# Constant rows in PSUM, six more gathered groups and one counted block less in a graph layer

## The chip, the cores and the metric

The kernel runs on one core of a Trainium2 chip. Its time is the device time of one execution in microseconds; a figure for a kernel is the median of several runs. A profile is one more execution, taken by the hardware profiler: its span runs from the first instruction to the last, and the execution itself is a little longer than that. Engines are named as in the profile: PE is TensorE (PEld its weight loads), DVE is VectorE, ACT is ScalarE, POOL is GpSimd, SP is SyncE, which issues most DMAs.

## What is computed

One graph layer with a residual. There are 6250 nodes of 64 features and 206250 edges, sorted by target node; W1 is 64x128, W2 is 128x64, all in float32.

```python
h = jnp.maximum(_layernorm(x, axis=-1), 0.0)
...
msg = node_feat[src] + edge_feat
agg = jax.ops.segment_sum(msg, dst, num_segments=node_feat.shape[0])
h = jax.nn.relu(agg @ W1 + b1)
return h @ W2 + b2
...
x = x + _L0_gnn_ref(h, edge_attr_64, src, dst, ...)
```

`node_feat` is the normalised `h` here. Each node has some 33 edges. The sum over edges of `h[src]` is the heavy part: it touches 206250 rows of `h` in no order.

## The kernel before

**Two ways to the sum of h.** For most nodes the kernel doesn't fetch rows of `h`. It counts: for a window of three nodes (128 slots of edges, `SLOTS`) it makes a matrix of how often each source node occurs, by a product of two matrices of ones and zeros. A source number is split into a low part (0 to 127) and a key (a high part, 49 values, beside which of the three nodes is meant, so `K` = 147 columns). `hot_lo` says which low part an edge has, `hot_key` which key; VectorE makes both by comparing the edges' numbers with a row of consecutive numbers, `iota_lo` and `iota_key` (line 858). TensorE multiplies them into `pc` in PSUM (line 868), and ScalarE moves `pc` to the ring of counts in SBUF (line 871). Then TensorE multiplies the counts by `h` itself, held in SBUF in 49 pieces, into `pv` (line 888), and VectorE adds `pv` to the sums of all nodes, `agg` (line 900).

For the last groups of edges (a group is 1024 edges) GpSimd gathers rows of `h` from a table in HBM by indirect DMAs (line 301), 128 rows each, which add the rows to the edges' own features in the tile `pfeat`; eight gathers make a group. There are `GP` = 20 such groups; they are worked in pairs. TensorE sums a pair by node (line 489) with a matrix of ones and zeros (`hotp`), ScalarE empties it, TensorE places it (line 508), and VectorE adds it to `agg` (line 473).

**Steps and blocks.** The counts run in steps: six windows in one step (`ST`), so six matmuls and one eviction. 14 steps are a block (84 windows, 252 nodes), and there are `NW` = 23 blocks, the last with `BL` = 56 windows (10 steps): 318 steps. Every third step opens a new pair of `hot_lo` and `hot_key`, with 18 windows each, in two buffers. In the first seven steps of a block the 49 products of the block before are dealt out, 5 to 8 a step (`PRODUCTS`); in step 11 they are added (`ADDED`). `pv` has two buffers in PSUM, `pc` two of two banks each, `bank` and `po` one each: all eight banks are used.

**Feature sums.** The edges' own features are summed apart, in chunks of 42 nodes, two chunks to a unit, three units to a block, behind the counts of steps 8, 11 and 14 (`SUMS`). VectorE makes `hot` a step ahead (line 427), 48 matmul records on TensorE sum the unit in `bank` (line 439), ScalarE empties it into `by_node` (line 442), which frees the features' buffers for the next load, and TensorE adds it to the next block's open `pv` (line 461). The layer for a block of 252 nodes (`mlp_hidden` and what follows) is dealt out over later steps.

**Order.** The order on every engine is the order in which the program records it; nothing reorders it later. A planner in the program decides behind which step a pair of gathered groups is summed. It has two clocks of its own: one of steps (`clock`, 1.25 us a step, `STEP_US`), one of GpSimd (`pool`, 2.3 us a gather by `GATHER_US`, 2.9 a fetch of words by `WORDS_US`). A pair is recorded in the first step of a block among 1, 2, 3 and 5 (`GROUPS`) where GpSimd's clock plus `LAND_US` is over. Four `pfeat` tiles hold two pairs, so the gathers of a pair wait until the pair two before it is summed. If the gathers come later than the planner has them, TensorE waits at the sum, with all that stands behind it.

**The opening.** Before the first step, the edges' sources are converted on ScalarE (line 589), transposed on TensorE (594), evicted (595) and packed with the targets by VectorE (598), then written to HBM. The first edges of each window are found by a search over gathered rows (lines 311 and 317). `by_quarters` turns the sources of the gathered groups for the gathers' indices, through `pv`'s buffers (651, 653): one quarter, then two, then the last ahead of the counts of step 4.

Of the kernel before, what the change touches and what calls it, by code (L numbers as in the profile page):

```python
# [55 lines left out]
GP = 20  # L56
# [20 lines left out]
NW = 23  # L77
BL = 56
# [32 lines left out]
GATHER_US = 2.3  # L111
WORDS_US = 2.9
# [9 lines left out]
def gnn_kernel(ctx: ExitStack, tc: tile.TileContext, x, src_t, dst_t, dst_g, edge, w1, b1, w2, b2, out):  # L122
# [278 lines left out]
    nc.vector.memset(bank, 0.0)  # L401
    units = []
# [29 lines left out]
    def chunk_sum(u):  # L432
        n = units[u][2]
        hot, feat = hot_of.pop(u), feats.pop(u)
        for i in range(n):
            for k in range(JP):
                for q in range(JQ):
                    j = q * JP + k
                    nc.tensor.matmul(bank[q * QP:q * QP + WQ, i * D:(i + 1) * D], hot[:, i, j, :], feat[i][:, j, :],  # L439
                                     start=(k == 0), stop=(k == JP - 1))  # L440
        by_node[u] = work.tile([P, GB, D], F32, name="by_node", bufs=3)
        nc.scalar.activation(by_node[u][:, :n].rearrange("p c d -> p (c d)"), bank[:, :n * D], AF.Copy)  # L442
        load(u + 2)
# [201 lines left out]
    def by_quarters(t0, t1):  # L645
        rows = src_s.bitcast(F32)
        for t in range(t0, t1):
            own = slice(t * QP, (t + 1) * QP)
            px = ps.tile([P, 512], F32, tag="pv", name="psrcq")[:, :GP * PK]
            for b in range(PQ):  # L650
                nc.tensor.matmul(px, spread[own, b].rearrange("p a c -> p (a c)"), rows[own, :, b, :],
                                 start=(b == 0), stop=(b == PQ - 1))
            nc.scalar.activation(src_p[:, :, t], px.rearrange("p (g k) -> p g k", k=PK), AF.Copy)
# [31 lines left out]
    junk = late.tile([P, RC * CT], BF16, name="junk")  # L685
# [159 lines left out]
    def count(b, s):  # L845
# [4 lines left out]
        if r == 0:  # L850
# [5 lines left out]
            for k, (hot, iota_k) in enumerate(zip(hots, (iota_lo, iota_key))):  # L856
# [18 lines left out]
    def open_pv(b):  # L875
        pvs[b] = [ps.tile([P, 512], F32, tag="pv", name="pv")[:, :BN], 0]
# [102 lines left out]
    def fetch_h(g):  # L979
# [4 lines left out]
        for j in range(J):  # L984
            queue.append((GATHER_US, lambda j=j: gather(
# [116 lines left out]
    PRODUCTS_L = (8, 18, 28, 39, HI)  # L1102
    ADDED, LOADED = 10, 2
    LAST, LATE, SUMS_L = (3, 8), 7, (6, 8)
# [13 lines left out]
    places = {}  # L1118


    for u, (b, c, _) in enumerate(units):
# [4 lines left out]
        at(n, chunk_sum, u)  # L1126
# [15 lines left out]
    for n, (b, s) in enumerate(steps):  # L1142
        for f in before.get(n, []):
            f()
        count(b, s)
# [3 lines left out]
        if b >= 1 and s == (PLACES if b < NW - 1 else 2):  # L1149
# [23 lines left out]
        if n >= 3:  # L1173
            if h_next < G and s in GROUPS and fetched.get(h_next + 1, 1e9) + LAND_US <= clock(n):
# [164 lines left out]
```

## Time and profile before

| | |
|---|---|
| median of 3 runs | 492.47 us (490.9 to 494.97) |
| profiled execution | 489.07 us |
| its span | 487.2 us |
| PE busy | 424.2 us, 87% |
| DVE busy | 415.1 us, 85% |
| POOL busy | 388.3 us, 80% |
| ACT busy | 366.0 us, 75% |
| DMA moved | 77.98 MB, 160 GB/s over the span |

TensorE's busy time is modelled: matmuls are pipelined, and records of one matmul overlap. An f32 matmul shows as two records. In rows of groups the columns are line, engine, operation, what is written from what, shapes and count, then busy us and mean ns of one, then the engine's idle time just before them with what ended most of it. In rows of the timeline they are the start and duration in us, then the same, with the idle time just before and its end in brackets.

### The profile page before, as it was taken

Reading aid. Unit: us, or ns where it says so; the run is one execution under the profiler, and the core shown is the slowest. Engines: PE = TensorE matmul, PEld = TensorE weight load, DVE = VectorE, ACT = ScalarE, POOL = GpSimd, SP = SyncE. Lnnn points to the kernel's source line nnn. Section 1 sums busy time; section 2 is a strip of 40 time slices with the busy share of each in tenths; the row PEclk is TensorE's granted clock in tenths of the full one; section 3 lists DMA queues with packets and bytes.
Section 4 is the critical chain, followed back from the end, with each engine's and each line's share of the span. In section 5 each row is a group of like instructions: output and inputs, shape, how many; then the busy total and the mean of one; then the engine's idle time right before and its main releaser. Section 6 shows DMA issues by size and latency. Waiting matters only on the chain.

```text
span 487.2 us, 17218 instructions
## 1 busy us (share of the span) xinstructions
PE 424.2 (87%) x7301; PEld 374.8 (77%) x7302; DVE 415.1 (85%) x561; ACT 366.0 (75%) x607; POOL 388.3 (80%) x239
## 2 busy tenths in 40 slices
PE   3156798998988999999999999989999999999894
PEld 3055687886886888888988978878888888888783
DVE  7888989879999798988998889888998899998751
ACT  3727889878877788788898789777887787786650
POOL 7787888888888888888888888888888888888000
PEclk9655699999999999999999999999999999999998
DMA  9959367378366585784784784675775775764700
GB/s 237 238 172 300 74 147 193 76 180 192 69 167 155 145 228 122 176 230 105 192 220 98 172 228 94 170 201 125 187 187 124 201 179 122 203 158 93 213 13 16
DMA packets 122378, 77.98 MB, mean 160 GB/s; under 512 B 34768, under 2 KB 120728, under 8 KB 122072
## 3 DMA queue, kind: packets, MB, share of 16 engines
q1 hardware_dynamic: 97464, 66.88, 47.1%
q0 software_dynamic: 24592, 9.19, 15.0%
q8 instruction: 59, 0.97, 0.8%
q10 hardware_dynamic: 240, 0.75, 0.5%
q14 instruction: 23, 0.19, 0.1%
HBM read 72.80 MB, written 3.99 MB: 158 GB/s over the span
## 4 chain that ended last, share of the span: by engine, by line
PE 68%; ACT 13%; DMA 6%; issue 5%; DVE 4%; POOL 3%; DVEq 0%; ACTq 0%; POOLq 0%
PE pv L888 26%; PE pc L868 22%; PE bank L439 11%; ACT counts L871 9%; POOL rows L301 3%; DMA feat<-in_edge 3%; PE po L943 2%; PE pv L461 2%; DMA dstq<-in_dst_g,cols_i 2%; ACT junk L694 1%; PE ph L936 1%; PE bank L489 1%; DVE hot_key L858 1%; DVE hot_lo L858 1%; DMA firsts_i<-in_dst_g 1%
## 5 line engine op out<-in xcount | busy, mean ns | idle before, releaser
L301 POOL DMA_INDIRECT pfeat<-table,src_p x160 | 334.0, 2088 | 49.7 <-issue 43.0
L871 ACT ACTIVATE counts<-pc 128x882 fp32r<-128x882 f32 x318 | 282.1, 916 | 49.1 <-PE pc L868 39.8
L868 PE MATMUL pc<-hot_key,hot_lo 128*128 128x147 bf16 x1908 | 179.2, 232 | 22.9 <-ACT counts L871 13.6
L858 DVE TENSOR_TENSOR hot_lo<-iota_lo,keys 128x2304 bf16<-128x2304 bf16 (+1 forms) x107 | 143.8, 1344 | 36.2 <-PE pc L868 29.0
L888 PE MATMUL pv<-counts,h 128*128 128x252 f32 (+1 forms) x1127 | 171.0, 292 | 0.2
L868 PEld LDWEIGHTS <-hot_lo 128*128 128x128 bf16 x1908 | 130.5, 100 | 45.4 <-issue 24.2
L858 DVE TENSOR_TENSOR hot_key<-iota_key,keys 128x2664 bf16<-128x2664 bf16 (+1 forms) x107 | 163.3, 1526 | 0.0
L888 PEld LDWEIGHTS pv<-counts,h 128*128 128x128 f32 x1127 | 143.5, 190 | 0.6 <-ACT counts L871 0.5
L439 PE MATMUL bank<-feat,hot 128*21 128x64 f32 x3240 | 69.0, 222 | 5.9 <-issue 3.0
L439 PEld LDWEIGHTS bank<-feat,hot 128*21 128x21 f32 x3240 | 52.3, 101 | 18.3 <-issue 6.8
L427 DVE TENSOR_TENSOR hot<-rel,iota 128x504 f32<-128x504 bf16 x68 | 45.6, 671 | 0.1
L442 ACT ACTIVATE by_node<-bank 128x128 f32<-128x128 f32 x68 | 19.0, 280 | 18.4 <-PE bank L439 12.4
L301 POOL DMA_INDIRECT words<-packed,first_i x15 | 20.8, 1385 | 4.6 <-issue 3.4
L301 POOL DMA_INDIRECT rows<-in_dst_g,row_i x15 | 17.4, 1162 | 5.2 <-issue 4.0
L943 PE MATMUL po<-w2s,hid 128*126 128x64 f32 (+2 forms) x100 | 16.8, 288 | 1.7 <-ACT hid L938 1.2
L943 PEld LDWEIGHTS po<-w2s,hid 128*126 128x126 f32 (+2 forms) x100 | 13.5, 192 | 5.7 <-ACT hid L938 1.9
L936 PE MATMUL ph<-sums,w1s 128*128 128x252 f32 (+2 forms) x50 | 16.1, 404 | 0.2 <-ACT y L949 0.2
L900 DVE TENSOR_TENSOR sums<-sums,pv 128x252 f32<-128x252 f32 (+4 forms) x31 | 9.8, 339 | 6.7 <-PE pv L888 5.9
L492 ACT ACTIVATE by_group<-bank 128x128 f32<-128x128 f32 x10 | 2.8, 277 | 15.1 <-PE bank L489 11.1
L938 ACT ACTIVATE hid<-ph,b1s 128x252 f32<-128x252 f32 (+2 forms) x25 | 11.6, 464 | 2.3 <-PE ph L936 2.3
L461 PE MATMUL pv<-select,by_node 128*64 128x42 f32 (+1 forms) x272 | 12.6, 234 | 0.0
L461 PEld LDWEIGHTS pv<-select,by_node 128*64 128x64 f32 x272 | 9.9, 137 | 3.0
(202 smaller groups left out, 252.3 us busy)
## 6 DMA issues: line engine op xcount, KB each, us to landing
feat<-in_edge SPq DMA_DIRECT2D x135, 384.0 KB
pfeat<-in_edge SPq DMA_DIRECT2D x20, 256.0 KB
pfeat<-table,src_p POOLq DMA_INDIRECT x160
xl<-in_x SPq DMA_DIRECT2D x2, 768.0 KB
xs<-in_x SPq DMA_DIRECT2D x23, 63.0 KB
out_y<-y SPq DMA_DIRECT2D x23, 63.0 KB
dstn<-in_dst_g SPq DMA_DIRECT2D x1, 1024.0 KB
table<-xl SPq DMA_DIRECT2D x1, 800.0 KB
```

The source lines that it names most:

```text
L301: nc.gpsimd.indirect_dma_start(out=rows, out_offset=None, in_=source, in_offset=bass.IndirectOffsetOnAxis(ap=index, axis=0), compute_op=op)
L427: nc.vector.tensor_tensor(hot_of[u][:, :n].rearrange("p c j w -> p (c j) w"), rel[:, c:c + n].rearrange("p c q k -> p (c q k)").unsqueeze( ...
L439: nc.tensor.matmul(bank[q * QP:q * QP + WQ, i * D:(i + 1) * D], hot[:, i, j, :], feat[i][:, j, :], start=(k == 0), stop=(k == JP - 1))
L442: nc.scalar.activation(by_node[u][:, :n].rearrange("p c d -> p (c d)"), bank[:, :n * D], AF.Copy)
L461: nc.tensor.matmul(pvs[b][0][i * D:(i + 1) * D, k:k + z - a], of[:, i, :], select[:, a - low:z - low], start=False, stop=False)
L858: nc.vector.tensor_tensor(hot[:, :n].rearrange("p t (m o) -> p t m o", o=2), iota_k.rearrange("p (m o) -> p m o", o=2).unsqueeze(1).to_bro ...
L868: nc.tensor.matmul(pc[:, k, m * K:(m + 1) * K], hot_lo[:, j, :], hot_key[:, j, :K], start=True, stop=True)
L871: nc.scalar.activation(ring[:, (2 * b + half) % 3, :, i * ST * V:(i + 1) * ST * V].rearrange("p h (k m) -> p h k m", k=2), pc[:, :, :ST // ...
L888: nc.tensor.matmul(pv[:, :2 * half].rearrange("p (k n) -> p k n", k=2), h2[:, h, :], of[:, :, h, :half], start=(h == 0), stop=(h == HI - 1))
L936: nc.tensor.matmul(ph[:, :n], w1s, agg[:, start[b]:start[b + 1]], start=True, stop=True)
L938: nc.scalar.activation(outs[b][:, :n], ph[:, :n], AF.Relu, bias=b1s)
L943: nc.tensor.matmul(po[:pairs[b], k, :], outs[b][:, k:2 * pairs[b]:2], w2s, start=True, stop=True)
```

## The change

**Constant rows.** A new PSUM tile `iotas` (bf16, one bank) holds the two rows of consecutive numbers that line 858 compares with. It is filled once, near the start: a matmul spreads a row over a column, ScalarE copies it to SBUF, a transpose puts it back as a row on all partitions; this three times. The comparisons then read `iotas` in PSUM in place of `iota_lo` and `iota_key` in SBUF. For its bank, `pv` goes from two buffers to one, in `open_pv` and in `by_quarters`.

**More gathered, fewer counted.** `GP` goes from 20 to 26, `NW` from 23 to 22 with the last block full (`BL` 84): 308 steps. Gathers whose edges all lie past the end of the list are left out (four, in the last group): 204 gathers in place of 160. `GATHER_US` goes from 2.3 to 1.6, `WORDS_US` from 2.9 to 1.2. A pair may also be summed in any step of the last block after the third. The last block's places for products, sums and layers become those of the other blocks, or later.

**Feature sums.** A unit's first chunk is summed ahead of its step's counts, the second where both were, behind them.

In the built program the 13 pairs stand behind 43, 58, 85, 100, 127, 143, 169, 187, 211, 229, 253, 271 and 295 steps; before, the ten stood behind 47, 85, 113, 142, 173, 211, 239, 271, 309 and the last in the drain.

```diff
-GP = 20
+GP = 26
...
-NW = 23
-BL = 56
+NW = 22
+BL = 84
...
-GATHER_US = 2.3
-WORDS_US = 2.9
+GATHER_US = 1.6
+WORDS_US = 1.2
...
     bank = ps.tile([P, GB * D], F32, name="bank", bufs=1)
     nc.vector.memset(bank, 0.0)
+    iotas = ps.tile([P, P + K + 1], BF16, name="iotas", bufs=1)
+    col = ps.tile([P, 3, P], F32, tag="pc", name="pcol")
+    cols_of = late.tile([P, 3, P], BF16, name="iota_cols")
+    m = K + 1 - P
+    for k, of in enumerate((iota_lo, iota_key[:, :P], iota_key[:, P:])):
+        n = of.shape[1]
+        nc.tensor.matmul(col[:n, k, :], of[0:1, :], onesb[0:1, :], start=True, stop=True)
+        nc.scalar.activation(cols_of[:n, k, :], col[:n, k, :], AF.Copy)
+        nc.tensor.transpose(iotas[:, k * P:k * P + n], cols_of[:n, k, :], identb[:n, :n])
...
-    def chunk_sum(u):
+    def chunk_sum(u, i):
         n = units[u][2]
-        hot, feat = hot_of.pop(u), feats.pop(u)
-        for i in range(n):
+        hot, feat = hot_of[u], feats[u]
+        if i < n:
             for k in range(JP):
...
+        if i < GB - 1:
+            return
+        hot_of.pop(u)
+        feats.pop(u)
         by_node[u] = work.tile([P, GB, D], F32, name="by_node", bufs=3)
...
-            px = ps.tile([P, 512], F32, tag="pv", name="psrcq")[:, :GP * PK]
+            px = ps.tile([P, 512], F32, tag="pv", name="psrcq", bufs=1)[:, :GP * PK]
...
-            for k, (hot, iota_k) in enumerate(zip(hots, (iota_lo, iota_key))):
+            for k, (hot, iota_k) in enumerate(zip(hots, (iotas[:, :P], iotas[:, P:]))):
...
-        pvs[b] = [ps.tile([P, 512], F32, tag="pv", name="pv")[:, :BN], 0]
+        pvs[b] = [ps.tile([P, 512], F32, tag="pv", name="pv", bufs=1)[:, :BN], 0]
...
         for j in range(J):
+            if g * P * J + j // PK * P * PK + j % PK >= E:
+                continue
...
-    PRODUCTS_L = (8, 18, 28, 39, HI)
+    PRODUCTS_L = PRODUCTS
     ADDED, LOADED = 10, 2
-    LAST, LATE, SUMS_L = (3, 8), 7, (6, 8)
+    LAST, LATE, SUMS_L = (5, 12), 11, SUMS
...
-        at(n, chunk_sum, u)
+        sum_first.setdefault(n, []).append(u)
+        at(n, chunk_sum, u, 1)
...
+        for u in sum_first.pop(n, []):
+            chunk_sum(u, 0)
         count(b, s)
...
-            if h_next < G and s in GROUPS and fetched.get(h_next + 1, 1e9) + LAND_US <= clock(n):
+            if h_next < G and (s in GROUPS or b == NW - 1 and s > LOADED) and fetched.get(h_next + 1, 1e9) + LAND_US <= clock(n):
```

More of the change, by code (lines that the diff above doesn't have):

```diff
@@ L684, in gnn_kernel @@
     sums_bad = bad[:, CHECKED + 2 * NT:]
-    junk = late.tile([P, RC * CT], BF16, name="junk")
+    junk = late.tile([P, max(RC * CT, 2 * GP * J)], BF16, name="junk")
     def checked(of, p, low, high, at):
@@ L1118, in gnn_kernel @@
     places = {}
+    sum_first = {}
     for u, (b, c, _) in enumerate(units):
@@ L1148, in gnn_kernel @@
             multiply(b - 1, upto[s])
-        if b >= 1 and s == (PLACES if b < NW - 1 else 2):
+        if b >= 1 and s == PLACES:
             for u in places[b - 1]:
```

## The prediction

> **What bounds the kernel now.** I read the page first (span, busy shares, chain, groups), then each engine's timeline around one block, then GpSimd's gathers against what VectorE ran beside them. The first rows are of the page, the last three of the view by windows (us, busy us and count of each engine, TensorE clock, DMA share, GB/s); the windows are the 22nd and 23rd counted block and the drain.
>
> ```profile
> span 487.2 us, 17218 instructions
> PE 68%; ACT 13%; DMA 6%; issue 5%; DVE 4%; POOL 3%; DVEq 0%; ACTq 0%; POOLq 0%
> L301 POOL DMA_INDIRECT pfeat<-table,src_p x160 | 334.0, 2088 | 49.7 <-issue 43.0
> L442 ACT ACTIVATE by_node<-bank 128x128 f32<-128x128 f32 x68 | 19.0, 280 | 18.4 <-PE bank L439 12.4
> ...
> 436.70:455.40 18.70, 16.96 (x299) 14.93 (x295) 16.46 (x19) 13.74 (x20) 12.98 (x6) 1.00 0.60 146
> 455.40:471.10 15.70, 15.43 (x273) 13.84 (x265) 8.64 (x14) 10.84 (x18) 0.00 (x0) 1.00 0.34 104
> 471.10:487.20 16.10, 9.71 (x107) 8.31 (x107) 2.71 (x11) 1.49 (x5) 0.00 (x0) 0.90 0.07 17
> ```
>
> TensorE's order sets the end, with VectorE close behind (17.0 and 16.5 of the 18.7 us of a full block). The last partial block costs 15.7 us and is what the change takes out. GpSimd is off the path: in the last two windows it does nothing. But it works without a pause until then: 160 gathers take 334.0 + 49.7 = 384 us, 2.40 each with the idle time before it. The change gives it 44 more, so its price per gather decides the case.
>
> **Price of a gather.** Timeline rows (start, duration): first GpSimd, then VectorE at the same moments.
>
> ```profile
> 12.54 1.79 POOL L301 DMA_INDIRECT rows<-in_dst_g,row_i  x1 [0.30 <-issue]
> 25.57 0.95 POOL L301 DMA_INDIRECT rows<-in_dst_g,row_i  x1 [0.30 <-issue]
> 45.43 1.59 POOL L301 DMA_INDIRECT pfeat<-table,src_p  x1 [1.30 <-ACT counts L871]
> 107.17 1.55 POOL L301 DMA_INDIRECT pfeat<-table,src_p  x1 [0.30 <-issue]
> 113.93 2.40 POOL L301 DMA_INDIRECT pfeat<-table,src_p  x1 [0.31 <-issue]
> 449.14 2.30 POOL L301 DMA_INDIRECT pfeat<-table,src_p  x1 [0.30 <-issue]
> ...
> 11.75 1.76 DVE L550 TENSOR_TENSOR xl<-xl,stat 128x1536 f32<-128x1536 f32 x1
> 22.92 3.47 DVE L557 TENSOR_REDUCE stat<-square 128x24 f32<-128x1536 f32 x2
> 108.79 1.36 DVE L858 TENSOR_TENSOR hot_lo<-iota_lo,keys 128x2304 bf16<-128x2304 bf16 x1 [2.75 <-issue]
> 113.56 1.36 DVE L858 TENSOR_TENSOR hot_lo<-iota_lo,keys 128x2304 bf16<-128x2304 bf16 x1 [1.03 <-PE pc L868]
> ```
>
> The gather at 107.17 had VectorE idle beside it (idle for 2.75 us until 108.79) and took 1.55. The one at 113.93 began while `hot_lo` ran (until 114.92) and ended 1.41 us after that: it was held until the VectorE instruction was over. Not every instruction does this: the `rows` gather at 25.57 ran inside two reduces, which have one input, and took 0.95; the one at 12.54, inside L550 with two SBUF inputs, took 1.79. So a `pfeat` gather costs 1.54 + 0.30 of issue = 1.84 when nothing holds it, and the hold is by VectorE instructions with two inputs in SBUF. After the change L858 reads its constant row from PSUM and has one SBUF input; I take its hold as gone. The Trainium skill (SBUF — State Buffer, section Who interferes with whom) says this too: VectorE reaches a second SBUF input through a read interface shared with GpSimd, and an instruction with at most one SBUF input does not contend. No row here has the case of one SBUF and one PSUM input under a gather; the reduces agree with it.
>
> What still holds a gather are the other two-input instructions. These are VectorE's rows by form:
>
> ```profile
> L858 DVE TENSOR_TENSOR hot_key<-iota_key,keys 128x2664 bf16<-128x2664 bf16 x105 | 161.6, 1539 | 0.0
> L858 DVE TENSOR_TENSOR hot_lo<-iota_lo,keys 128x2304 bf16<-128x2304 bf16 x105 | 142.3, 1355 | 36.0 <-PE pc L868 29.0 <-issue 3.6 <-ACT counts L871 1.8
> L427 DVE TENSOR_TENSOR hot<-rel,iota 128x504 f32<-128x504 bf16 x67 | 45.2, 675 | 0.1
> L928 DVE TENSOR_TENSOR xs<-xs,b2s 126x128 f32<-126x128 f32 x23 | 6.5, 282 | 0.0
> ```
>
> L427 runs 45.2 of the 406 us between the first and the last gather (45.43 to 451.44), 11%, and holds a gather that meets it for 0.34 on average: 0.037 per gather. L928 and its like add 0.01. With 192 gathers (why 192, below) this is 9 us; its bounds are 0 and 15.
>
> **The change, part by part.** *A block less, six groups more.* Before, 318 steps; after, 308, all blocks full. What was the start of the last block then becomes the drain. On TensorE:
>
> ```profile
> 406.73 0.65 PE L489 MATMUL bank<-pfeat,hotp 128*21 128x64 f32 x32
> 407.31 0.56 PE L868 MATMUL pc<-hot_key,hot_lo 128*128 128x147 bf16 x6
> 407.67 1.07 PE L888 MATMUL pv<-counts,h 128*128 128x252 f32 x7
> ...
> 453.19 0.55 PE L868 MATMUL pc<-hot_key,hot_lo 128*128 128x147 bf16 x6 [0.61 <-ACT counts L871]
> ...
> 473.17 4.37 PE L888 MATMUL pv<-counts,h 128*128 128x180 f32 x37
> ...
> 481.87 0.29 DVE L959 TENSOR_TENSOR y<-po,xs 122x128 f32<-122x128 f32 x1 [1.46 <-PE po L943]
> ```
>
> Step 308's counts end at 453.74. Behind them the new drain has half a sum, 49 products of 252 columns at 1.07/7 = 0.153 (7.5 us; before, 49 of 180 columns at 4.37/37 = 0.118, 5.8), placing, two layers, and the 5.0 us from 482.16 to the end: about 17.3 us, where the old drain from its last counts (470.2) took 17.0. So TensorE's own pace gives 453.7 + 17.3 = 471.0. The three more pairs of groups put 0.65 each on TensorE and 0.33 for placing: +2.9.
>
> *The opening.* The three rows of constants are made on TensorE and ScalarE: three times a matmul, a ScalarE copy, a transpose, each behind the last. In the built order they stand on TensorE behind the `pf` matmuls and on ScalarE ahead of the conversion of `src`. Also, `pv` has one buffer instead of two, and `by_quarters(1, 3)` takes two at once.
>
> ```profile
> 8.90 0.17 PE L287 MATMUL pf<-in_hw,less 128*128 128x15 bf16 x1
> 8.92 3.70 PE L594 MATMUL psrc<-ident,src 128*91 128x128 f32 x16
> 33.51 2.80 PE L651 MATMUL psrcq<-src_s,spread 32*128 32x40 f32 x16
> ...
> 5.17 1.42 ACT L589 ACTIVATE src<-src 128x1456 f32<-128x1456 int32 x1 [1.47 <-DMA src<-in_src_t]
> 10.96 2.05 ACT L595 ACTIVATE srcl<-psrc 91x1024 int32<-91x1024 f32 x1 [4.37 <-PE psrc L594]
> 36.25 0.31 ACT L653 ACTIVATE src_p<-psrcq 128x40 int32<-128x40 f32 x2
> 36.45 2.90 ACT L578 ACTIVATE h<-xl 128x1536 fp32r<-128x1536 f32 x2
> 39.25 0.91 ACT L871 ACTIVATE counts<-pc 128x882 fp32r<-128x882 f32 x1
> ```
>
> The conversion, done at 6.6 now, then starts behind the third copy: 9.0 plus three rounds of about 0.2 (matmul) + 0.28 (a 128x128 copy from PSUM, the `by_node` row) + 0.1 is 10.7, and ends at 12.1. TensorE's `psrc` moves from 8.92 to 12.1: 3.2 late, and ScalarE is nearly gapless from 10.96 to the counts, so this stays. The second quarter's matmuls (1.4 of the 2.80) must now wait for the first's eviction at 36.25: ScalarE's copies of `h` and the counts behind them move 1.6 more. Together 4.8, bounds 0 (if gaps absorb it) and 6. The gathers wait for the last of these evictions, behind the first counts, so they move too: from 45.4 to 50.2.
>
> *The sums in two halves.* The same 48 matmuls, half of them ahead of the step's counts, so that ScalarE gets a bank to empty sooner. In steps 8 to 14 of a block ScalarE, at 0.91 a step, is the slower of the two; per block 0 to 0.6 us can go, 0.3 taken, 6 over 20 blocks. Against it: `hot` and its features are wanted a step's counts earlier.
>
> *The single buffer of `pv`* costs nothing later: a block's products are added in step 11 and the next block's open four steps on. The instructions of gathers that are skipped (four past the end of the list) are counted out: 204, not 208.
>
> **Where the gathers meet TensorE.** In the built order the sums of the gathered pairs stand behind fixed steps, and TensorE waits there, with all later counts queued behind. The row at 406.73 is the eighth pair of before, behind step 271: it needs 128 gathers. After the change the twelfth pair stands behind step 271 and needs 192. GpSimd also has 13 other fetches by then.
>
> ```profile
> 43.19 0.94 POOL L301 DMA_INDIRECT words<-packed,first_i  x1 [0.30 <-issue]
> ...
> q0 software_dynamic: 52, 0.01, 2.5%
> ```
>
> The second row is the DMA view of 455 to 460 us: 52 packets of GpSimd's queue there, though its last gather ended at 451.44, so landing takes over 3.5 us; I take 3.5. The sum: 50.2 + 192 x 1.84 (353.3) + 9 of holds + 13 x 1.25 (16.3) = 428.8 for the 192nd gather, 432.3 landed, 433.0 with the pair's sum. TensorE, at its own pace, would be there at about 407.3 + 4.8 + 4 (four more pairs by then, 0.98 each) - 6 = 410, so it stands still for some 22 us, spread over pairs eight to twelve. From step 272's counts to the last counts it took 407.31 to 453.74 = 46.4; with the thirteenth pair (1.0) and the gain of the halves (1.0) the same. It needs 12 gathers more, 23 us, and comes 30 us on, so it isn't late. Then 433.0 + 46.4 + 17.3 = 496.7 span. The profiled execution took 489.07 for a span of 487.2, 1.9 outside it: 498.6. The median of the runs, 492.47, is 3.4 above the profiled time; I set 500.
>
> Bounds: with no holds and an unmoved opening 496.7 - 9 - 4.8 = 483 span; with holds of 15, an opening of 6 and slower steps (19 a block) about 505.
>
> **Rivals.**
> *TensorE is not held up.* Then 471.0 + 2.9 + 4.8 - 6 = 472.7 span (467 to 479), 476 against the median, 3% faster. For it: the whole expected gain is there, and the other GpSimd fetches cost 1.25 instead of 1.84. Against it: 192 gathers must have landed by 410, that is (410 - 3.5 - 16.3 - 50.2)/192 = 1.77 each with issue, holds and all, less than the lowest row, 1.84. Chance 0.27, for an error in my chain of starts, landings and waits.
>
> *VectorE falls to one element a cycle.* L858's two forms differ by 360 elements and 184 ns, 0.51 ns an element; L427 and L928, at 4 bytes, by 376 elements and 393 ns, 1.05 with 148 fixed. If a PSUM operand takes the fast rate away, the two cost 2.56 + 2.93 = 5.5 us in three steps instead of 2.9. VectorE's other work is 16.5 - 14/3 x 2.9 = 3.0 a block, so it needs 14/3 x 5.5 + 3.0 = 28.7 where a block has 18.7: 10 more, some 700 us in all. This decides once the two pass (18.7 - 3.0) x 3/14 = 3.4 us in three steps. The Trainium skill (VectorE: DVE Perf Modes, The perf-mode tier table) has `tensor_tensor` with any PSUM operand at 1x, which would give this time; the paragraph below it, on why PSUM drops a tier, still allows the packed 16-bit mode. No row here has a 16-bit PSUM operand. Chance 0.08.
>
> *The hold stays* though the row lies in PSUM, so the change doesn't do what it says: 2.40 a gather, 50 + 192 x 2.40 + 20 = 531, + 4 + 64 = some 600. Chance 0.08.
>
> **How the numbers follow.** The forecast, TensorE waiting for gathers, has 0.52 (488 to 509 by itself); 0.05 is for waits that I haven't seen. About 1% is what a measurement can tell here: 487.5 to 497.4 is no change. Of the forecast's 0.52 some 0.19 lies there, 0.03 below it by the lower bounds, 0.30 above. Faster 0.27 + 0.03 = 0.30; same 0.19; slower 0.30 + 0.16 + 0.05 = 0.51. The two heavy cases are left out of the range and it reaches down into the fast one: 472 to 509.
>
> **What would show it.** In the profile after: `pfeat` gathers near 1.6 mean, GpSimd without a pause until about 450, L858 at 1.36 and 1.54; first counts on ScalarE near 44 instead of 39.25; gaps of TensorE ahead of the gathered sums of pairs eight to twelve, released by the gathers' DMA, some 20 us in sum. Gathers under 1.5, no such gaps, or an L858 at 2.5 would each prove me wrong.

## The result and the profile after

The changed kernel takes 509.37 us in the median (507.48 to 513.51, four runs) beside 492.89 for the kernel before on the same chip: ratio 1.0345, 95% interval 1.0267 to 1.0423. It is slower, as forecast, and its time lies 0.4 us above the range. The profiled execution has a span of 507.0 us where the one before has 487.2. Some executions of a kernel take 1.5 to 3.5% longer than its fastest; ratios and their intervals leave these out, and the profiles of e5 and e10, marked with a star in the table below, are of such longer executions.

First the page of the changed kernel (the span, two rows of its 40 slices, two groups), then two rows of its groups by form, then one of its groups by line. A group's columns: busy us, mean ns of one, idle time just before them and what ended it. Lines moved by 13: the counts' matmul is L881 now, their eviction L884, VectorE's one-hots L871, the feature sums L448, their eviction L455, the pairs' sums L502.

```profile
span 507.0 us, 17112 instructions
...
POOL 8677888858888888887888888888888888860000
PEclk9755699999999899997999989999899999999998
...
L301 POOL DMA_INDIRECT pfeat<-table,src_p x204 | 322.1, 1579 | 66.7 <-issue 56.4
L884 ACT ACTIVATE counts<-pc 128x882 fp32r<-128x882 f32 x308 | 275.4, 920 | 76.0 <-PE pc L881 63.2
```

```profile
L871 DVE TENSOR_TENSOR hot_key<-iotas,keys 128x2664 bf16<-128x2664 bf16 x101 | 155.0, 1534 | 0.0
L871 DVE TENSOR_TENSOR hot_lo<-iotas,keys 128x2304 bf16<-128x2304 bf16 x101 | 136.8, 1354 | 58.9 <-PE pc L881 45.1 <-issue 5.8 <-PE pk L731 2.2
```

```profile
L502 PE MATMUL bank<-pfeat,hotp 128*21 128x64 f32 x416 | 9.9, 242 | 0.1
```

The GpSimd side came as forecast: 204 gathers at 1.58 us instead of 160 at 2.09, without a pause, VectorE's one-hots at their old 1.35 and 1.53 us. (Of GpSimd's 66.7 us of idle time ahead of the gathers 56.4 are the 0.3 us of issue ahead of each.) The 192nd gather ends at 430.0 us (428.8 forecast). But the last row has TensorE waiting 0.1 us in all ahead of the gathered sums, not 22. It came too late to wait: by the first matmul of each block's counts, 20 blocks (the second to the twenty-first) take 20.33 us each, where the kernel before took 18.73. That is 32 us more; the opening adds 4.5, and the block less takes 16 off, which leaves the 20 us between the two spans.

Two of these rows say where: ScalarE's idle time ahead of the counts is 76.0 us, and VectorE's ahead of `hot_lo` 58.9 (36.0 before), both put down to TensorE's counts. ScalarE's row on the page of before:

```profile
L871 ACT ACTIVATE counts<-pc 128x882 fp32r<-128x882 f32 x318 | 282.1, 916 | 49.1 <-PE pc L868 39.8
```

A timeline of one such wait in the changed kernel (start, duration, engine):

```profile
200.96 0.53 PE L448 MATMUL bank<-feat,hot 128*21 128x64 f32 x24
...
201.43 0.56 PE L881 MATMUL pc<-hot_key,hot_lo 128*128 128x147 bf16 x6
...
201.58 1.54 POOL L301 DMA_INDIRECT pfeat<-table,src_p  x1 [0.30 <-issue]
...
201.92 0.53 PE L448 MATMUL bank<-feat,hot 128*21 128x64 f32 x24
...
202.89 0.92 ACT L884 ACTIVATE counts<-pc 128x882 fp32r<-128x882 f32 x1 [1.37 <-PE bank L448]
```

The first half of a feature sum is issued at 200.96, the counts behind it at 201.43, and by these rows the counts end at 201.99. ScalarE has nothing else to do and starts on them at 202.89, 0.90 later. In between lies a gather, from 201.58 to 203.12; ScalarE is let go 0.23 ahead of its end. (A TensorE row's end is modelled; the start of the reader is not.) TensorE's semaphore events, the signals by which it tells other engines that a piece of work is done, say the same: the one for the half sum comes at 201.54, on time, the one for the counts behind it at 202.86.

In what follows an eviction is called late by its start minus the later of two ends: that of its last matmul's row, and that of ScalarE's instruction before. Summed where over 0.15 us, the counts are 0.8 us late in the profile of before and 29.6 (38 of 308) in the one after; the feature sums' evictions are 10.0 and 10.8 us late. So the lateness grew by 29.5 us, from 10.8 to 40.3, while the blocks lost 32. That is a correlation, and where the lateness comes from is what the runs had to find.

### The profile page after: what moved, and what is told of

Read it like the earlier page. It is cut to its first block, busy times and chain, and to the rows that moved or that the text cites. A ratio compares the mean times of both kernels' runs of the same rounds, so it can differ in the third digit from the quotient of the medians.

```text
span 507.0 us, 17112 instructions
## 1 busy us (share of the span) xinstructions
PE 436.4 (86%) x7200; PEld 372.3 (73%) x7201; DVE 407.7 (80%) x563; ACT 352.6 (70%) x605; POOL 370.5 (73%) x283
## 5 line engine op out<-in xcount | busy, mean ns | idle before, releaser
L301 POOL DMA_INDIRECT pfeat<-table,src_p x204 | 322.1, 1579 | 66.7 <-issue 56.4
L884 ACT ACTIVATE counts<-pc 128x882 fp32r<-128x882 f32 x308 | 275.4, 920 | 76.0 <-PE pc L881 63.2
L881 PE MATMUL pc<-hot_key,hot_lo 128*128 128x147 bf16 x1848 | 178.4, 233 | 15.1 <-ACT counts L884 8.9
L871 DVE TENSOR_TENSOR hot_lo<-iotas,keys 128x2304 bf16<-128x2304 bf16 (+1 forms) x104 | 139.2, 1339 | 60.2 <-PE pc L881 46.2
L901 PE MATMUL pv<-counts,h 128*128 128x252 f32 x1078 | 166.9, 296 | 6.8 <-ACT counts L884 6.1
L871 DVE TENSOR_TENSOR hot_key<-iotas,keys 128x2664 bf16<-128x2664 bf16 (+1 forms) x104 | 157.7, 1517 | 0.0
L881 PEld LDWEIGHTS <-hot_lo 128*128 128x128 bf16 x1848 | 128.1, 100 | 40.3 <-issue 19.8
L448 PE MATMUL bank<-feat,hot 128*21 128x64 f32 x3144 | 77.2, 224 | 7.5 <-issue 5.2
L448 PEld LDWEIGHTS bank<-feat,hot 128*21 128x21 f32 x3144 | 51.0, 101 | 27.4 <-issue 9.2
L455 ACT ACTIVATE by_node<-bank 128x128 f32<-128x128 f32 x66 | 18.4, 278 | 11.2 <-PE pc L881 7.1
L301 POOL DMA_INDIRECT words<-packed,first_i x15 | 14.6, 970 | 4.6 <-issue 4.6
L956 PE MATMUL po<-w2s,hid 128*126 128x64 f32 (+2 forms) x100 | 17.2, 294 | 0.8 <-ACT hid L951 0.6
L913 DVE TENSOR_TENSOR sums<-sums,pv 128x252 f32<-128x252 f32 (+2 forms) x29 | 9.5, 347 | 7.6 <-PE pv L901 7.6
L949 PEld LDWEIGHTS ph<-sums,w1s 128*128 128x128 f32 x50 | 7.7, 195 | 6.5 <-issue 4.1
L474 PE MATMUL pv<-select,by_node 128*64 128x42 f32 x262 | 12.1, 235 | 0.0
```

Of the source, the lines that this page charges most:

```text
L301: nc.gpsimd.indirect_dma_start(out=rows, out_offset=None, in_=source, in_offset=bass.IndirectOffsetOnAxis(ap=index, axis=0), compute_op=op)
L474: nc.tensor.matmul(pvs[b][0][i * D:(i + 1) * D, k:k + z - a], of[:, i, :], select[:, a - low:z - low], start=False, stop=False)
L871: nc.vector.tensor_tensor(hot[:, :n].rearrange("p t (m o) -> p t m o", o=2), iota_k.rearrange("p (m o) -> p m o", o=2).unsqueeze(1).to_bro ...
L881: nc.tensor.matmul(pc[:, k, m * K:(m + 1) * K], hot_lo[:, j, :], hot_key[:, j, :K], start=True, stop=True)
L884: nc.scalar.activation(ring[:, (2 * b + half) % 3, :, i * ST * V:(i + 1) * ST * V].rearrange("p h (k m) -> p h k m", k=2), pc[:, :, :ST // ...
L901: nc.tensor.matmul(pv[:, :2 * half].rearrange("p (k n) -> p k n", k=2), h2[:, h, :], of[:, :, h, :half], start=(h == 0), stop=(h == HI - 1))
```

## The experiments

The runs came in six groups, each on a chip of its own. On three chips the kernel before takes 470 us, on three 492 to 495, as on the chip of the first pair. These are called chips of 470 and of 490; each run is compared with the kernel before on its own chip. All numbers of blocks are means of the same 20 blocks.

### First group: the halves, the pairs' places, the rows (a chip of 470)

Theory 1 was that the half sums ahead of the counts cost TensorE its pace; theory 2 that something else of the change did.

```
-        for u in sum_first.pop(n, []):
-            chunk_sum(u, 0)
...
+        at(n, chunk_sum, u, 0)
         at(n, chunk_sum, u, 1)
```

> The changed kernel with each feature sum whole again, both chunks behind its step's counts. Theory 1 (the halves ahead of the counts cost TensorE its pace, 1.5 us a block): blocks of 18.7 us come back, and then TensorE does arrive ahead of the gathers, near 410 us at the twelfth pair, and waits some 20 us for them: span 493 to 499. Theory 2 (the pace is lost to something else of the change: the rows in PSUM, the single buffer of pv, six more groups): blocks stay at 20.3, no waits for gathers, span 504 to 510.

Measured: ratio 1.058 (1.053 to 1.063), span 494.3. The view of waits (who, for what, us in all, times, longest):

```profile
PE pc L881 <- ACT counts L884: 19.0, 27, 2.3
PE bank L502 <- DMA pfeat<-table,src_p: 18.1, 11, 3.2
```

Here TensorE does wait for gathers, 18.1 us in 11 matmuls. Four of the 20 blocks take 23.8 to 26.6 us, the other sixteen 18.4 in the mean. This is the forecast's mechanism, and its span to 2.4 us, though on a chip whose blocks are shorter than those that the forecast was worked out from. It looked like theory 1.

```
-GATHER_US = 1.6
+GATHER_US = 1.8
```

> As the one before, and the planner's price of a gather 1.8 instead of 1.6, so that the gathered pairs stand further back in TensorE's order (the twelfth behind step 302). Theory 1: blocks of 18.7 and no waits for gathers, opening +4.5, a block less, three pairs more: span 476 to 482, faster than both kernels. Theory 2: span 502 to 510, since the pace isn't in the sums' place.

Ratio 1.000 (0.997 to 1.003), blocks of 18.16, span 468.0. The waits are gone, but it is not faster. The chain of the work that ended last, near its end (start, us, what), shows why:

```profile
442.42 1.55 POOL pfeat L301
444.36 1.82 issue
446.18 1.55 POOL pfeat L301
448.03 1.58 POOL pfeat L301
449.92 1.23 POOL pfeat L301
451.77 1.26 POOL pfeat L301
453.62 3.35 DMA pfeat<-table,src_p
```

From 402 us on the chain runs through GpSimd. The last counts end at 445.3, the last gather at 455.2, and the drain has to wait for its landing. With 26 groups GpSimd sets the end wherever TensorE is quick.

Then two parts of the change alone, on the kernel before: the halves as in the change's diff, and the rows in PSUM with one buffer of `pv`.

> The kernel before with the sums' first chunk ahead of the counts, and nothing else of the change. Theory 1: 1.5 us a block more over 22 blocks, up to +33 us: 510 to 525. Theory 2: the halves cost nothing or gain a little: 486 to 494.

> The kernel before with the rows of numbers in PSUM and one buffer of pv, nothing else. Theory 1: the opening alone, +4.5 us (495 to 499), blocks of 18.7; gathers of 1.55 in the mean. Theory 2, in the form that the rows or the single buffer slow the steps: 510 to 525.

The halves: 1.008 (1.005 to 1.011), blocks of 18.14. The rows: 1.011 (1.007 to 1.015), blocks of 18.05, first counts 4.6 us later than in the halves' run on TensorE. On this chip neither costs pace, and no run on it has more than 1.1 us of late evictions. Theory 1 has fallen, on this chip at least: the halves alone cost 3.8 us, where it wanted 18 or more.

### Second group: the two kernels again (a chip of 490)

> The kernel before once more, for a profile of it beside the others on one chip. No theory speaks of it: about 470 us if this chip is as the last four runs had it, about 492 if it is as the first pair had it; its blocks then take 18.0 or 18.7 us.

> The changed kernel once more. Theory 1 (the halves themselves cost 1.5 us a block): has fallen, since the halves alone cost 0.8% and whole sums were slower still. Theory 3: in the changed kernel TensorE waits for gathers wherever its pace allows, and the sums' halves hardly matter: ratio 1.04 to 1.06, span that of the run with whole sums (494) within 4 where the chip gives blocks of 18.0, with single waits of 5 to 8 us ahead of gathered sums in four or five blocks. Theory 4: the halves do cost pace in this company (tight gathers, single pv): blocks of 19.5 to 20.4 everywhere, no waits for gathers, ratio 1.03 to 1.04.

> The changed kernel with its halves and the planner's price of a gather 1.8, which puts the twelfth pair behind step 302. Theory 3: waits for gathers go, ratio 0.995 to 1.01, as with whole sums. Theory 4: the pace stays at 19.5 to 20.4 a block, ratio 1.03 to 1.04.

The kernel before took 491.69 in the median here (486.87 to 503.51). The changed kernel has ratio 1.017 (1.010 to 1.024) with blocks of 19.80 and 3.6 us of waits for gathers; with the pairs put back 1.009 (1.004 to 1.013) with blocks of 19.49. Neither theory 3 nor 4 is met: putting the pairs back gains a little, the pace stays lost. The new thing is the lateness: 28.2 and 32.2 us in these two, where the first group never had over 1.1. This gave theory 5: the lateness is a given of the chip, which the halves pass on to the counts.

### Third group: whole sums where they are late (a chip of 490)

> The changed kernel with whole sums and the pairs put back (price 1.8), once more, beside the two below. Theory 5: on some chips TensorE ends the feature sums 0.3 to 3 us later than it issues them; with whole sums behind the counts only the sums' own eviction comes late, with a half ahead of the counts ScalarE's evictions of the counts come late too (30 us in the first profile after, 20 and 17 in the next two, none in the kernel before). So, if the kernel before takes about 490 on the chip that this meets: ratio 0.965 to 0.985, counts' evictions late by under 2 us in sum. If it takes about 470, where the sums aren't late: 1.00 as measured. The rival (the lateness belongs to the whole changed kernel): ratio 1.00 to 1.02 on a chip with 490.

> As the one above, and the rows of numbers made behind the turning of src, with their three products side by side and two copies instead of a chain of three; the quarters of src in the buffers of pc, so that one needn't wait for the other's eviction. The opening's 4.5 us should go: first counts 3 to 4.5 us earlier than in the run above, ratio 0.006 to 0.01 lower.

The edit of e9, besides one line that puts the quarters of `src` into the buffers of `pc`:

```
+    for k, of in enumerate(ofs):
+        nc.tensor.matmul(col[:of.shape[1], k, :], of[0:1, :], onesb[0:1, :], start=True, stop=True)
+    nc.scalar.activation(cols_of[:, :2], col[:, :2], AF.Copy)
+    nc.scalar.activation(cols_of[:m, 2], col[:m, 2], AF.Copy)
```

> The kernel before with the halves alone, once more. Theory 5: 1.008 again where the kernel before takes 470; where it takes about 490, 17 to 33 us more, ratio 1.03 to 1.07, the counts' evictions late by that sum. The rival: 1.00 to 1.01 on either chip.

Theory 5 fell on both sides. e8, without halves, 1.038 (1.031 to 1.045), blocks of 20.61, 36.9 us late, now mostly on the sums' own evictions. e10, halves on the kernel before, 0.992 (0.986 to 0.998). The lateness goes with the changed kernel, halves or not. e9 did what it should: first counts 3.8 us earlier on TensorE, ratio 0.006 lower, though the two intervals overlap (1.026 to 1.038 for e9).

The same kernel on the two kinds of chip (e8 here, e2 above), each with a whole feature sum of 48 matmul records that runs into a gather. First e8:

```profile
377.32 0.87 PE L448 MATMUL bank<-feat,hot 128*21 128x64 f32 x48
377.88 1.54 POOL L301 DMA_INDIRECT pfeat<-table,src_p  x1 [0.30 <-issue]
...
379.45 0.28 ACT L455 ACTIVATE by_node<-bank 128x128 f32<-128x128 f32 x1 [1.06 <-PE pc L881]
```

Then e2:

```profile
247.02 0.91 PE L448 MATMUL bank<-feat,hot 128*21 128x64 f32 x48
...
247.55 1.55 POOL L301 DMA_INDIRECT pfeat<-table,src_p  x1 [0.30 <-issue]
...
248.27 0.28 ACT L455 ACTIVATE by_node<-bank 128x128 f32<-128x128 f32 x1 [0.18 <-PE bank L448]
```

On the chip of 490 the eviction starts 1.26 us after the sum's row ends (378.19), just as the gather ends (379.42). On the chip of 470 it starts 0.34 us after (0.18 after ScalarE came free), in the middle of the gather. TensorE's semaphore events give this for all the half sums. (Not every event is in the traces, 682 for 766 signalling instructions in the profile after, so they are matched in order.) Take the half sums whose rows end between 1.5 and 0.4 us ahead of the end of a gather of under 1.65 us. In the profile after all 50 were signalled over 0.2 us late, 49 of them in the gather's last 0.3 us, in the median 0.20 ahead of its end; in e8 all 62 were late, in e2 4 of 60.

Counts are held too, less often. Of those whose rows end in that stretch, in the profile after, 29 of 30 were late behind a late half sum, 9 of 26 behind one on time, as in the first timeline, and 11 of 46 elsewhere; in e2 none of 150.

Gathers held by VectorE, as in the kernel before, stop the sums for less of their time. Of the half sums whose rows end in a gather of over 1.9 us, 25 of 65 were late in the profile before. 10 of the 25 were signalled 0.4 to 0.6 us ahead of the gather's end and most others 1.4 to 2.2 us ahead, none between. That the free stretch between is the one in which VectorE holds the gather would fit, but isn't shown. This is theory 6: on these chips a gather stops the feature sums, and an unheld one does it for longer.

### Fourth group: without gathers, unheld, held (a chip of 490)

e11 puts nothing in the place of a gather; e13 lets VectorE read the rows from SBUF again; e14 drops the addition.

```
-            queue.append((GATHER_US, lambda j=j: gather(
-                parts_of[g][:, j, :], table[:, :], src_p[...], OP.add)))
+            queue.append((GATHER_US, lambda: None))
```

> The changed kernel without its 204 gathers of the second part (their source rows are left out of the output); everything else issues as before. Theory 6: on chips where the kernel before takes 490, a gather stops TensorE's feature sums from its start until 0.2 us before its end (in the profiles there, every half sum that should end in that stretch of a short gather ended at its last 0.2 us). So without gathers the sums end when they should, on any chip: no eviction of counts late, blocks of 18.0 to 18.3, span 455 to 470. The rival (these chips are late with the sums anyway, from transfers or their clock): blocks of 19.5 to 20.4 where the kernel before takes 490.

> The kernel before with the rows of numbers in PSUM and one buffer of pv, once more. Theory 6: where the kernel before takes 490 its gathers, no longer held by VectorE, now stop the sums for 1.3 us in one piece instead of two shorter ones, so the sums end later (middle of a half sum 0.5 to 0.7 us late instead of 0.3) and a block costs 0.5 to 1.5 more: ratio 1.03 to 1.07, of which 1.01 is the opening. Where it takes 470: 1.011 again. The rival (the lateness comes from the six more groups): 1.01 on either chip.

```
-            for k, (hot, iota_k) in enumerate(zip(hots, (iotas[:, :P], iotas[:, P:]))):
+            for k, (hot, iota_k) in enumerate(zip(hots, (iota_lo, iota_key))):
```

> The changed kernel with VectorE reading the rows of numbers from SBUF again (the rows in PSUM are still made), so that the gathers are held again. Theory 6: sums as little late as in the kernel before (middle 0.3), a gather 2.1 in the mean, the 192nd near 515, TensorE waits for the gathers at pairs eight to twelve: span 560 to 600. The rival (lateness has to do with the rows in PSUM or with TensorE's order, not with how long a gather is held): middle 0.6, the span the same.

> The changed kernel with gathers that write the fetched rows over the loaded ones instead of adding them (the sum of the two is left out). The plain gathers of the opening took 0.95 us instead of 1.54, with as many rows. Theory 6, in the form that GpSimd's instruction stops the sums and not its transfers: the stretch is shorter by 0.6 us, so the sums are less late (middle under 0.3), ends 0.2 us ahead of the gather's end again, blocks of 18.5 to 19.2 where the kernel before takes 490. If the transfers do it: lateness as with adding, blocks of 19.5 or more.

The groups of the sums' evictions, in e11, then e12, then e4 (the kernel of e12 on the chip of 470), with the gathers of the last two:

```profile
L455 ACT ACTIVATE by_node<-bank 128x128 f32<-128x128 f32 x66 | 18.8, 284 | 0.0
```

```profile
L301 POOL DMA_INDIRECT pfeat<-table,src_p x160 | 253.1, 1582 | 141.9 <-issue 43.7 <-PE pc L877 41.4 <-DMA pfeat<-in_edge 38.8
...
L451 ACT ACTIVATE by_node<-bank 128x128 f32<-128x128 f32 x68 | 19.0, 279 | 42.2 <-PE pc L877 20.9 <-PE bank L448 18.6 <-PE po L952 1.8
```

```profile
L301 POOL DMA_INDIRECT pfeat<-table,src_p x160 | 252.3, 1577 | 108.0 <-issue 43.0 <-DMA pfeat<-in_edge 26.1 <-PE pc L877 21.1
...
L451 ACT ACTIVATE by_node<-bank 128x128 f32<-128x128 f32 x68 | 19.4, 285 | 4.2 <-PE bank L448 3.7 <-PE pc L877 0.3
```

Without gathers ScalarE never waits for a feature sum (0.0 us idle ahead of the evictions), blocks take 18.66, one of them 23.9, and the ratio is 0.964 (0.959 to 0.970), where the changed kernel with its gathers has 1.017 and 1.0345 on two other chips of 490. One of 129 half sums is over 0.2 us late. What the table below has as late is one wait of ScalarE of 4.2 us in the block of 23.9, whose end the profile doesn't explain. Blocks and span (474.5, 4.5 above the expected stretch) are longer than theory 6 had them. With 160 unheld gathers and nothing else of the change but the rows (e12) the idle time ahead of the sums' evictions is 42.2 us, with blocks of 20.06 and a ratio of 1.043 (1.037 to 1.048); on the chip of 470 it is 4.2 us, and the ratio 1.011. Neither the halves nor the six groups are needed for the loss. With the gathers held again (e13) a half sum is signalled 0.16 us after its row's end in the median, where it is 0.20 in the profile before, 0.48 in e12, 0.50 in the profile after and 0.05 in e11 and e4. The evictions are late by 17.1 us in all instead of 32.6 to 40. And, as expected, the kernel starves for gathers, so that e13 differs from the changed kernel in more than the hold:

```profile
PE bank L502 <- DMA pfeat<-table,src_p: 60.0, 26, 4.5
```

Its ratio is 1.164 (1.156 to 1.173, two runs). e14 tells nothing of its question: ahead of its gathers GpSimd waited 194.2 us for the loads of `pfeat`, TensorE waited in turn, it took 727.88 us, and only 5 of its half sums ended inside a gather. Whether the instruction or its transfers stop the sums stays open.

### Fifth and sixth group: gathers beside the sums (two chips of 470)

e15 is the kernel before with the rows made as in e9. In e16 and e17 GpSimd was also to wait for each feature sum (the kernel before has 68, not the 66 of the text below). The lines that make the wait, and the planner's:

```
+        for hot in summed:
+            nc.gpsimd.memset(hot[0:1, 0, 0, 0:1], 0.0)
+            pool[0] = max(pool[0], clock(n) + PAUSE_US)
...
-            pool_until(clock(n) + LAND_US)
+            pool_until(clock(n) + AHEAD_US)
```

> The kernel before with the rows of numbers in PSUM, made behind the turning of src as in e9, and nothing else. Beside the run below. Where the kernel before takes 490: the gathers are not held, they stop the sums, ratio 1.02 to 1.045, evictions of the sums late by 25 to 35 us in all. Where it takes 470: 0.995 to 1.005.

> As the one above, and GpSimd waits for each of the 66 feature sums before it goes on with gathers (a store of one word into the sum's used one-hot, which must wait for the sum), the gathers planned at 1.72 with no look ahead, so that 5, 1 and 1 of them lie between the sums. Theory 6: the gathers are as many and as short, but no longer beside the sums, so the sums are not late: evictions of the sums late by under 6 us in all, blocks of 18.0 to 18.5 where the kernel before takes 490, ratio 0.965 to 0.99 (one pair more in the drain costs some 2 us). If the sums are late for another reason that goes with short gathers: evictions late as above, ratio 1.02 or more.

> As e16, with the gathers planned at 1.5 and the pauses at 1.1, which puts 6, 1 and 1 of them between the sums, eight in a block instead of seven, so that few are left for the drain. Theory 6, where the kernel before takes 490: blocks of 18.0 to 18.5, evictions of the sums late by under 6 us in all, ratio 0.965 to 0.995. Where it takes 470: blocks of 18.0, ratio 1.00 to 1.01 (GpSimd's pauses bring nothing there). If the sums are late for another reason that goes with short gathers: ratio 1.02 or more where the kernel before takes 490.

> As e15, beside the run above on one chip: where the kernel before takes 490, ratio 1.02 to 1.045 and evictions of the sums late by 25 to 35 us; where it takes 470, 0.998 again.

Both groups ran on chips of 470. e15 and e18: 0.999 (0.996 to 1.001) and 1.001 (0.999 to 1.004). e16 keeps blocks of 18.03, but at seven gathers a block it has some left at the end: last counts at 451.7, last gather at 489.5, ratio 1.072 (1.067 to 1.077). e17, eight a block, is at 1.001 (0.999 to 1.003). So the pauses cost nothing with eight.

But the store does not wait for the whole sum, as these expectations have it. It touches one word of the first chunk's part of `hot`, and in the traces it starts 0.35 us after the sum's start in the median; of the 65 sums that show 48 records in one piece it starts in all ahead of the sum's end. In e17, for one, a sum runs from 271.32 to 272.19 by its rows, the store is done at 271.76, and the next gather starts at 271.91. In 46 of the 65 the next gather starts before the sum's row ends (in e16 in 50). Gathers still overlap the sums for 17.2 us, where it is 39.5 in e18, and the sums' evictions are later than without the pauses, 7.8 us in all against 0.5. So gathers that keep clear of the sums have not been tried on any chip, and these pauses not on a chip of 490.

The runs side by side; late is the lateness of both kinds of evictions in the profiled execution:

| run | kernel | chip | gathers, mean us | late us | us a block | ratio |
|---|---|---|---|---|---|---|
| before | before | 490 | 160, 2.09 | 10.8 | 18.73 | 1 |
| after | changed | 490 | 204, 1.58 | 40.3 | 20.33 | 1.0345 |
| e1 | changed, whole sums | 470 | 204, 1.58 | 0.6 | 19.73 (waits for gathers) | 1.058 |
| e2 | and pairs put back | 470 | 204, 1.59 | 0.8 | 18.16 | 1.000 |
| e3 | before, halves | 470 | 160, 2.10 | 0.0 | 18.14 | 1.008 |
| e4 | before, rows | 470 | 160, 1.58 | 1.1 | 18.05 | 1.011 |
| e5* | before | 490 | 160, 2.09 | 22.4 | 19.39 | (its median 491.69) |
| e6 | changed | 490 | 204, 1.58 | 28.2 | 19.80 | 1.017 |
| e7 | pairs put back | 490 | 204, 1.58 | 32.2 | 19.49 | 1.009 |
| e8 | as e2 | 490 | 204, 1.58 | 36.9 | 20.61 | 1.038 |
| e9 | as e2, rows later | 490 | 204, 1.57 | 34.6 | 20.40 | 1.032 |
| e10* | as e3 | 490 | 160, 2.10 | 16.5 | 18.84 | 0.992 |
| e11 | changed, no gathers | 490 | none | 4.2 | 18.66 | 0.964 |
| e12 | as e4 | 490 | 160, 1.58 | 32.6 | 20.06 | 1.043 |
| e13 | changed, rows in SBUF | 490 | 204, 1.95 | 17.1 | 23.63 (waits for gathers) | 1.164 |
| e14 | changed, plain gathers | 490 | 204, 0.96 | not comparable | 30.27 (waits for loads) | (one run, 727.88) |
| e15 | before, rows later | 470 | 160, 1.58 | 0.2 | 18.03 | 0.999 |
| e16 | and pauses | 470 | 160, 1.56 | 9.0 | 18.03 | 1.072 |
| e17 | as e16, eight a block | 470 | 160, 1.57 | 7.8 | 18.08 | 1.001 |
| e18 | as e15 | 470 | 160, 1.58 | 0.5 | 18.03 | 1.001 |

## Why the prediction was wrong

**The step that failed** is TensorE's own pace: "TensorE, at its own pace, would be there at about 407.3 + 4.8 + 4 (four more pairs by then, 0.98 each) - 6 = 410, so it stands still for some 22 us, spread over pairs eight to twelve". It carried 18.7 us a block over from the kernel before, as if the hold of the gathers concerned VectorE and GpSimd alone. The runs showed a third party: on chips of 490 the gathers stop TensorE's feature sums (without gathers, in e11, one half sum of 129 is late), and a held gather stops them for less of its time. With the gathers unheld a block costs 20.33 us, TensorE reaches the pairs 13 us and more after their gathers' ends, and no wait is left.

In spans: TensorE's old pace with the new drain makes 471.0; the forecast added 4.8 for the opening and 21 more (22 of waits, 4 for pairs, 6 off for the halves, 1 in rest), which is 496.7; measured are 4.5 and 32, which makes 507.5 for the 507.0 of the profile. Of the 32 some 3 are the work of three more pairs. That the rest is the sums' lateness rests on the sizes, 29.5 for some 29, and on e11 and e12, where taking gathers out removes the loss and leaving them unheld in the kernel before makes it; how much of it the half clock adds (last section) was not measured by itself.

**Price of a gather: right.** 1.84 with issue was forecast, 1.58 + 0.30 measured. The 127 gathers that start beside an instruction of L871 take 1.55 in the mean; before, the 98 beside L858 took 2.33. The 192nd gather came within 1.2 us. VectorE at one element a cycle, which the Trainium skill (VectorE: DVE Perf Modes, The perf-mode tier table) has for `tensor_tensor` with any PSUM operand, did not come: 1354 and 1534 ns against 1355 and 1539. Here the measurement decides against the table.

**TensorE waits for gathers: the mechanism is real, on other chips.** e1 has it, 18.1 us of waits and 494.3 of span, where the blocks without waits take 18.4; in the profile after the row of L502 shows 0.1 us.

**The halves: small, and of either sign.** 0.3 us a block, 6 in all, were to be gained. On the kernel before, e10 gained 0.8% on a chip of 490, 4 us, and e3 lost 0.8% on one of 470. What they do with unheld gathers is open: e7 with them has 1.009 and e8 without them 1.038, on two chips. The price set against them, "`hot` and its features are wanted a step's counts earlier", is not in the profile after, where TensorE waits for neither (in e10 it waits 5.9 us for features). In its place late sums reached the counts through them (29.6 us in the profile after), but without halves as much lateness falls on the sums' own evictions (29.0 of e8's 36.9).

**The opening: right in kind, short by 1.** ScalarE's rows of the changed kernel:

```profile
10.82 1.36 ACT L602 ACTIVATE src<-src 128x1408 f32<-128x1408 int32 x1
14.21 3.88 ACT L608 ACTIVATE srcl<-psrc 88x1024 int32<-88x1024 f32 x2 [2.03 <-PE psrc L607]
...
42.13 0.22 ACT L666 ACTIVATE src_p<-psrcq 128x52 int32<-128x52 f32 x1 [2.04 <-issue]
...
45.04 1.70 ACT L884 ACTIVATE counts<-pc 128x882 fp32r<-128x882 f32 x2
```

The first counts start at 45.04 instead of 39.25, 5.8 us where 4.8 stood (bounds 0 and 6); `srcl` moves 3.25, as worked out, and the second quarter's eviction is the rest: it comes 2.25 behind the first, where 1.6 stood, as its matmuls take 1.95 us instead of 1.4, for 52 columns instead of 40. e9 showed that 3.8 of it on TensorE can be had back. That the single buffer of `pv` costs nothing later holds too: e18 has it, at 1.001.

**A block less: right, but not free to be had.** The drain after the last counts took 17.0 us, 17.3 forecast. On the chip of 470, where the sums are hardly late (0.8 us) and no wait is left, e2 still gains nothing: 26 groups' gathers end at 455.2 and set the end themselves. The rival that TensorE is not held up, 3% faster, had left this out; it asked only whether the gathers come in time for pair twelve. In the profile after its condition holds, with 0.1 us of waits, and its 472.7 of span still doesn't come: it went by the same pace as the forecast.

The forecast of slower was right, then, but with one mechanism in the place of another. That 496.7 came as near to 507.0 as it did is luck: the two prices happen to be alike.

## What to carry to other kernels

A wait between two engines that goes may have shielded a third: before a hold is priced at its full length, look in the trace for whom it kept the held engine away from. A matmul's row has a modelled end; that its result is there is told by its signal and by when its reader starts, so sum the readers' lateness over the kernel and compare. An engine that is made to wait by touching a tile waits only for the users of the part that it touches, so look in the trace when it was let go. And a change that trades engines' overlaps has to be measured on more than one chip, here 1.00 on one and 1.04 on another for the same kernel.

## What the runs showed of the hardware

- On three of the six chips, and on that of the first pair, a GpSimd gather with addition holds back the end of TensorE's feature sums (48 short matmul records of 64 columns in 0.87 us) until some 0.2 us ahead of the gather's end: 50 of 50 half sums in the profile after, 62 of 62 in e8. Counts in that stretch were late in 49 of 102 cases in the profile after (pairs' sums aside), mostly behind a late half sum, products in none of 9. On the chips of 470 it hardly shows (4 of 60 half sums in e2, 5 of 51 in e4). Whether the matmuls stand still or only tell of their end later, whether the gather's instruction or its transfers do it, and why the chips differ, no run here shows. The Trainium skill (SBUF — State Buffer, Who interferes with whom) has it of the engines' SBUF ports that "PE and ACT never wait on anyone"; whether the sums and the gather meet in SBUF or elsewhere is open too.
- Right after a stop of TensorE the granted clock can fall to half. The view by windows of e5 (us, busy and count of PE, PEld, DVE, ACT, POOL, clock, DMA share, GB/s):

```profile
168.50:170.50 2.00, 1.96 (x61) 1.49 (x59) 1.67 (x3) 1.17 (x2) 1.70 (x2) 1.00 0.19 16
170.50:172.40 1.90, 1.32 (x13) 0.91 (x11) 0.00 (x0) 0.00 (x0) 1.59 (x2) 1.00 0.47 135
172.40:173.70 1.30, 0.11 (x2) 0.11 (x2) 1.23 (x1) 1.25 (x3) 0.99 (x2) 0.98 0.84 259
173.70:177.10 3.40, 3.40 (x62) 2.98 (x61) 2.18 (x3) 1.97 (x5) 3.10 (x2) 0.50 0.66 153
```

  VectorE and ScalarE stand still for 1.9 us, TensorE after them, and then it runs at 0.50 for 3.4 us. The profile after has four such stretches behind the opening, 17 us in all, each within 0.7 us of the end of a gap of 0.6 to 1.7 us in TensorE's rows; the one before has none there. At half speed that is up to 8.5 of the 32 us, an estimate. The Trainium skill (TensorE: Matmul & The Clock Gate, The HAM clock gate) has windows of about 3.4 us, and the lengths agree, 3.4 us three times and 6.8 once in the profile after. TensorE's rows are empty for 1.7 us at the most ahead of these falls, not for a whole window; whether its true idle time was longer than its rows show, no run tells.
- VectorE's two-input instruction with one bf16 input in PSUM and one in SBUF keeps its time (1354 ns against 1355) and does not hold GpSimd: the mean gather went from 2.09 to 1.58 us, with nothing else of the change but the rows in e4 and e12 too.
